# Seven products of combined quarters for the queries of a graph attention, and softmax sums turned by way of DRAM

## The chip, the core and the metric

The kernel runs on one core of one Trainium2 chip, in float32 throughout. The metric is the time on the device in microseconds (us), the median of several runs. A core has a matrix engine (PE, TensorE), a vector engine (DVE, VectorE), an engine for activation functions (ACT, ScalarE), a general engine (POOL, GpSimd) and one that here only issues DMA transfers (SP, SyncE). Each works through its own queue of instructions in order; semaphores tie them together. TensorE writes to PSUM, [...]from which VectorE and ScalarE read.

## The reference

There are 16 graphs (B) of 1024 nodes (N) with 256 channels (C), one 1024 x 1024 adjacency for all, and two layers with residuals. Cut to what matters:

```python
# layer 0: attention whose queries come from a weighted sum over neighbours
fea = transpose(relu(layernorm(x)))                     # (C, N) per graph
diff = c_adj[:, None, :] - c_adj[:, :, None]            # c_adj: mean over channels
A = abs(abs(sigmoid(diff) - 0.5) - 0.5) * 2.0           # symmetric
g = relu(einsum('bcn,bnm->bcm', fea, adj * A) * para)   # queries, 4 heads of 64
k, v = split((h @ kv_w))
x = x + softmax(q @ k.T * scale) @ v

# layer 1: graph convolution and two-layer perceptron with batch norms
deg = sum(A_norm, 0) + sum(A_norm, 1) - diagonal(A_norm)
agg = (A_norm * dinv[:, None] * dinv[None, :]) @ relu(layernorm(x))
y = relu(batchnorm(agg @ W1.T + b1))                    # over all graphs' nodes
x = x + batchnorm(y @ W2.T + b2)
```

The change concerns two places: the sum over neighbours `fea @ (adj * A)`, for each graph a product of 256x1024 by 1024x1024, and the division by the softmax's sums.

## The kernel before, in words

There are two stages. `layers` goes through the 16 graphs and ends with the perceptron's first half stored to DRAM (`y1_d`) and the residual (`x1_d`). `second` computes the batch norms over all graphs, the perceptron's second half and the output.

**One graph in the first stage.** `Norm` makes h_a, nodes on partitions, eight blocks of 128 nodes x 256 channels, and the channel sums csum. `columns_of` and `broadcast_row` spread those sums along a row (cbc, L181 to L193, called by `differences`). `transposed` makes ht, channels on partitions (L343 to L355). `weigh` (L363) makes the weighted adjacency in eight blocks w of 128 x 2 x 512: per block two Abs on ScalarE (L394), one Tanh (L402), and one operation on VectorE that adds one and multiplies with the block adj loaded from DRAM (L381). It is a generator of 17 slots; a block is spread over three of them. `queries` (L407) then takes, for each of two halves of 512 columns, 4 pairs of row blocks and 2 halves of channels, one piece each of four matmul instructions (`product`, L145 to L149: two half-width matmuls of 64 columns of weights). The sums of a column half gather in two PSUM banks, and are multiplied by para (L432) and put through relu (L435). `keys_values` makes keys and values from ht in eight pieces.

**Attention.** A unit is a pair of heads (k) and a half of the query nodes (f): four units per graph, 64 in all. A unit has four steps. Each step computes scores for two blocks of keys (L704), ScalarE's exponentials (L712), VectorE's running sum of the exponentials (acc, L731 and L734) and, one step later, the values' products o (L745). At a unit's end, two matmuls with a tile of ones (L762) sum acc over the partitions, with each head's sums repeated in 64 partitions; `divide` takes the reciprocals of that 128x512 tile in four pieces (L771) and multiplies with os, the copy of o (L774). Two steps later `finish` transposes os (L798), and adds it to the residual x (L802). Two reductions over the reciprocals (L777, L778) keep extremes in `seen`, from which the kernel tells whether a more careful version of the first stage (`layers(True)`) has to follow; it doesn't here.

**The order of the work.** `attention` writes it out by hand. Its 16 steps per graph are padded with pieces of other work from a generator, `background(b)`: while graph b attends, the queries, keys and values of graph b+1, the aggregation and the perceptron's first half of graph b-1, and the preparation of graph b+2 are issued. Every piece yields its cost in us of TensorE (1.71 for a piece), and after each step pieces are issued until the graph's `total` times the share of steps done is reached. `weave` puts one slot of a side generator behind each piece of the main one, `soon` puts an operation behind the next piece, and `TOP` stops until the scores of the next step are issued. `AHEAD` is the number of slots of `weigh` that are issued before the queries begin, in `prepare` three beside each of two groups of y pieces. `keys_values`, `queries`, `aggregate`, `hidden` and the transposes all take their PSUM from one pair of banks (`bank`, tag "mm").

`aggregate` (L489) already computes its product by seven products of combined quarters: fixed combinations of the normalized adjacency are made once, in `graph()` during graph 1, and kept in DRAM (`aht_d`); blocks of them are fetched three pieces ahead. `hidden` evicts the py banks to y on ScalarE (L564), stores y by a DMA that GpSimd issues (L565) and takes its statistics on VectorE (L568). `quarters` and `combine` (L474, L481) make two of the combinations of h_b.

**Buffers.** The pools are rings. There are four adj, w, p, q, k, v and y tiles, three of x and ht, two of acc, os, para and cb, and one of inv.

Of the kernel before, what the change touches and what calls it, by code (L numbers as in the profile page):

```python
# [17 lines left out]
P = 128  # L18
# [5 lines left out]
def gnn_two_layers_kernel(  # L24
# [36 lines left out]
    w2 = const.tile([P, HC, C], F32, name="w2")  # L61
# [11 lines left out]


# [10 lines left out]
    def layers(shifted):  # L85
# [12 lines left out]
        p3 = st.enter_context(tc.tile_pool(name=f"p3_{kind}", bufs=3))  # L98
        p4 = st.enter_context(tc.tile_pool(name=f"p4_{kind}", bufs=4))
# [41 lines left out]

        def bank(name):
            return ps_mm.tile([P, FB], F32, tag="mm", name=name)
# [15 lines left out]
        def load_adj(q, th, name):  # L159
            t = p4.tile([P, TH, FB], F32, tag="adj", name=name)  # L160
            nc.sync.dma_start(
                out=t,
                in_=adj[th * TH * P : (th + 1) * TH * P, q * FB : (q + 1) * FB].rearrange(
                    "(t p) m -> p t m", p=P
                ),
            )
            return t
# [4 lines left out]
        dbc = big.tile([P, N], F32, name="dbc")  # L172
        w1 = big.tile([P, CC, H1], F32, name="w1")
        rows = big.tile([P, NH, NT], F32, name="rows")

        def columns_of(col, name):

            cbs = []
            for g in range(NT // 4):
                cb = p2.tile([P, 4, P], F32, tag="cb", name=f"cb_{name}_{g}")  # L180
                nc.vector.tensor_copy(  # L181
                    cb, col[:, 4 * g : 4 * g + 4].unsqueeze(2).to_broadcast([P, 4, P])
                )
                cbs.append(cb)
# [10 lines left out]
        def load_adj_t(t, name):  # L195
            tile_ = p4.tile([P, N], F32, tag="adj", name=f"{name}_{t}")
# [3 lines left out]
        deg_sm = big.tile([P, 6, NT], F32, name="deg")  # L200
        row, diag, col, deg, tmp_deg, dinv = (deg_sm[:, i, :] for i in range(6))

        def degrees():

            nc.sync.dma_start(out=w1, in_=w1_t.rearrange("(k p) j -> p k j", p=P))
            nc.sync.dma_start(out=w2, in_=w2_t.rearrange("(k p) c -> p k c", p=P))
# [14 lines left out]
        def graph():  # L221
# [3 lines left out]
            for t in range(HT):  # L225
                for part in range(2):
                    cols = slice(part * HB, (part + 1) * HB)
                    a = p4.tile([P, 2, NH, HB], F32, tag="adj", name=f"au_{t}_{part}")
# [134 lines left out]
        def weigh(b):  # L363
# [11 lines left out]
            for slot in range(2 * NH * NP + 1):  # L375
# [11 lines left out]
                if not odd and i < NH * NP:  # L387
# [3 lines left out]
                    w = p4.tile([P, TH, FB], F32, tag="w", name=f"w_{b}_{q}_{th}")  # L391
# [13 lines left out]
        AHEAD = 6  # L405

        def queries(b):  # L407

            h = hs["a", b]
            qs[b] = [p4.tile([P, N], F32, tag="q", name=f"q_{b}_{k}") for k in range(CC)]  # L410
            for q in range(NH):
                cols = slice(q * FB, (q + 1) * FB)
                pgs = [bank(f"pg_{b}_{q}_{k}") for k in range(CC)]
                paras = []
                for k in range(CC):
                    paras.append(p2.tile([P, FB], F32, tag="para", name=f"para_{b}_{q}_{k}"))
                    nc.sync.dma_start(out=paras[k], in_=para[k * P : (k + 1) * P, cols])
                for th in range(NP):
                    i = q * NP + th
                    for k in range(CC):  # L420
                        for j in range(TH):
                            t = th * TH + j
                            product(
                                pgs[k],
                                h[:, t, k * P : (k + 1) * P],
                                weighted[b][i][:, j, :],
                                t == 0,
                                t == NT - 1,
                            )
                        if th == NP - 1:  # L430
                            dst = qs[b][k][:, cols]
                            nc.vector.tensor_mul(dst, pgs[k], paras[k])  # L432

                            soon(
                                lambda dst=dst: nc.scalar.activation(  # L435
                                    dst, dst, AF.Relu, scale=SCALE
                                )
                            )
                        yield 1.71
# [34 lines left out]
        def quarters(b):  # L474


            h = hs["b", b]
            HT = NT // 2
            return [h[:, n * HT : (n + 1) * HT, c * P : (c + 1) * P] for c in (0, 1) for n in (0, 1)]

        def combine(b):  # L481


            a11, a12, a21, a22 = quarters(b)
            s1s[b] = p1.tile([P, NT // 2, P], F32, tag="s1", name=f"s1_{b}")
            nc.vector.tensor_add(s1s[b], a21, a22)
            nc.vector.tensor_sub(a21, a11, a21)

        def aggregate(b):  # L489
# [5 lines left out]
            def load(upto):  # L495
                while len(pieces) <= min(upto, 7 * NP // 2 - 1):
                    i, th = divmod(len(pieces), NP // 2)
                    i = order[i]
                    a = p4.tile([P, TH, FB], F32, tag="adj", name=f"aht_{b}_{i}_{th}")
# [3 lines left out]
            load(2)  # L503
            yield 0.0
            a11, a12, a21, a22 = quarters(b)
            s1 = s1s[b]
# [18 lines left out]
            for i, (left, after) in enumerate(  # L525
# [11 lines left out]
                for th in range(NP // 2):  # L537
                    n = i * NP // 2 + th
                    load(n + 3)
# [35 lines left out]
        def normed(b):  # L575
# [3 lines left out]
            combine(b)  # L579
# [4 lines left out]
        def normed_last():  # L584
# [6 lines left out]
            combine(B - 1)  # L591
            nc.gpsimd.dma_start(out=x1_d[B - 1], in_=xs[B - 1])

        def prepare(b, products):
# [8 lines left out]
            for k in range(CC):  # L603
                yield from weave(islice(products, 3), (0, islice(w, 3)))
# [5 lines left out]
        endings = []  # L610

        def background(b):

            nothing = iter(())
            if b == 0:
                yield from prepare(1, nothing)
                yield from weave(queries(1), (0, weighers[1]), (1, degrees()))
                cbs = columns_of(dinv, "deg")
                if B > 2:
                    load_x(2)  # L620
                    yield from weave(keys_values(1), (1, Norm(2, True).all()))
                else:
                    yield from keys_values(1)
                yield TOP
                broadcast_row(dbc, cbs, "deg")
                yield 1.0
                if B > 2:
                    yield from prepare(2, nothing)
# [3 lines left out]
            if b + 1 < B:  # L632
                whole = graph() if b == 1 else nothing
                yield from weave(queries(b + 1), (0, weighers[b + 1]), (0, whole))
# [81 lines left out]
        class Unit:  # L716


            def __init__(self, b, k, f):
                self.at = (b, k, f)  # L720
                self.name = f"{b}_{k}_{f}"
                self.acc = None
                self.later = []
# [32 lines left out]
            def divide(self):  # L756

                b, k, f = self.at
                self.pt = ps_t.tile([P, FB], F32, tag="t", name=f"sums_{self.name}")
                for e in range(2):  # L760
                    r = slice(e * HD, (e + 1) * HD)
                    nc.tensor.matmul(  # L762
                        self.pt[r, :], ones, self.acc[:, e, :], start=True, stop=True
                    )
                self.inv = p1.tile([P, FB], F32, tag="inv", name=f"inv_{self.name}")
                u = (b * CC + k) * NH + f

                def invert(half):
                    for j in range(2 * half, 2 * half + 2):
                        c = slice(j * P, (j + 1) * P)  # L770
                        nc.vector.reciprocal(self.inv[:, c], self.pt[:, c])  # L771

                def scale():
                    nc.vector.tensor_mul(self.os, self.os, self.inv)  # L774

                def watch():
                    nc.vector.tensor_reduce(seen[:, 0, u : u + 1], self.inv, AX.X, ALU.max)  # L777
                    nc.vector.tensor_reduce(seen[:, 1, u : u + 1], self.inv, AX.X, ALU.min)  # L778

                invert(0)  # L780
                self.later = [lambda: invert(1), scale]
                self.watch = watch

            def behind_piece(self):
# [425 lines left out]
```

## Time and profile before

The median is 2698.26 us, of three runs from 2697.56 to 2699.33. The profiled execution spans 2698.1 us. What the chain that ended last consists of, by line:

| part of TensorE's work | line | share of the span |
|---|---|---|
| scores | L704 | 18% |
| values | L745 | 18% |
| queries (pg) | L149 | 16% |
| aggregation (pa) | L149 | 13% |
| perceptron, first half (py) | L149 | 7% |
| perceptron, second half (m_f) | L1017 | 7% |
| keys, values (pk, pv) | L149 | 4% each |
| sums, output's transposes | L762, L798 | 2%, 1% |

A group's line in the profile reads: line, engine, operation, output <- inputs with their shapes, count; busy us and mean ns of one; idle time of the engine just before them and what ended it. PE is TensorE, PEld its weight loads. A chain is followed back from the last instruction to what released each. In a table of windows each row gives a stretch of the span in us and the busy time of each engine in it.

Other durations that count: a row or column operation on 128x512 float32 takes VectorE 0.68 to 0.69 us, whether from PSUM or from SBUF; one on 128x1024 1.21 to 1.23; a ScalarE copy of 128x512 from PSUM 0.585, a pair of exponentials 1.94. The y stores land 2.8 us after their issue, the 512 KB adj blocks 4.2, the 1 MB yin blocks 6.3.

### The profile page before, as it was taken

What the parts mean: (1) busy time and instruction counts of PE and PEld (TensorE: products, weight loads), DVE (VectorE), ACT (ScalarE), POOL (GpSimd) and SP (SyncE); (2) the same over time, 40 slices, a digit from 0 to 9 for tenths busy, and PEclk for the clock granted to TensorE, in tenths of its full rate; (3) what the DMA queues carried; (4) which work ended last, traced back from release to release, by engine and by line L of the source; (5) the groups of instructions that cost most, each with busy time, mean ns of one, the idle gap of its engine ahead of it and who ended that gap; (6) DMA issues with size and microseconds to landing.
All of it is one profiled execution on the core that took longest, in us unless ns stands there. A gap on an engine that the chain in (4) does not pass through costs nothing.

```text
span 2698.1 us, 32021 instructions
## 1 busy us (share of the span) xinstructions
PE 2620.7 (97%) x12106; PEld 968.3 (36%) x12106; DVE 1742.3 (65%) x2624; ACT 1292.3 (48%) x1845; POOL 363.2 (13%) x428
## 2 busy tenths in 40 slices
PE   7999999999999999999999999999999999989994
PEld 3333333333333333333333333333333333324443
DVE  5767666666666656666666666566666666656675
ACT  5653444536363544445363635444453634335544
POOL 0016000000000100000000001000000001026653
PEclk9999999999999999999999999999999999999997
DMA  4416414243332424142423324241424213355549
GB/s 156 159 58 225 161 53 164 86 148 103 107 116 98 141 80 158 51 168 83 150 100 109 114 98 141 84 155 51 168 82 152 99 63 118 113 215 187 202 182 364
DMA packets 128613, 355.05 MB, mean 132 GB/s; under 512 B 11969, under 2 KB 32961, under 8 KB 122305
## 3 DMA queue, kind: packets, MB, share of 16 engines
q1 hardware_dynamic: 109120, 278.44, 30.3%
q0 software_dynamic: 19328, 74.46, 7.3%
q8 instruction: 98, 1.61, 0.2%
q14 instruction: 67, 0.54, 0.1%
HBM read 278.41 MB, written 74.45 MB: 131 GB/s over the span
## 4 chain that ended last, share of the span: by engine, by line
PE 93%; DMA 3%; DVE 2%; issue 2%; ACT 1%; POOL 0%; SPq 0%; POOLq 0%; DVEq 0%; ACTq 0%
PE sc L704 18%; PE o L745 18%; PE pg L149 16%; PE pa L149 13%; PE py L149 7%; PE m_f L1017 7%; PE pk L149 4%; PE pv L149 4%; PE sums L762 2%; DMA out_dram<-xo_f 2%; PE ot L798 1%; PE htp L352 1%; PE cbp_c L192 1%; DMA y_d<-y 0%; DVE acc L734 0%
## 5 line engine op out<-in xcount | busy, mean ns | idle before, releaser
L712 ACT ACTIVATE p<-sc 128x1024 f32<-128x1024 f32 x512 | 496.4, 1021 | 700.8 <-PE sc L704 700.6
L734 DVE TENSOR_TENSOR acc<-acc,p 128x1024 f32<-128x1024 f32 x384 | 471.2, 1227 | 133.8 <-ACT p L712 112.5
L704 PE MATMUL sc<-q,k 64*128 64x512 f32 x2048 | 510.6, 617 | 0.5 <-ACT p L712 0.5
L745 PE MATMUL o<-p,v 128*64 128x512 f32 x2048 | 496.1, 605 | 0.0
L149 PE MATMUL pg<-w,h_a 128*64 128x512 f32 x2048 | 457.1, 596 | 7.5 <-DVE q L432 7.5
L149 PE MATMUL pa<-aht,h_b 128*64 128x512 f32 x1536 | 346.0, 592 | 2.7 <-DMA aht<-aht_d 2.7
L704 PEld LDWEIGHTS sc<-q,k 64*128 64x128 f32 x2048 | 176.6, 186 | 321.9 <-issue 270.3
L149 PEld LDWEIGHTS pg<-w,h_a 128*64 128x64 f32 x2048 | 148.2, 138 | 301.8 <-issue 281.7
L771 DVE RECIPROCAL inv<-sums 128x128 f32<-128x128 f32 x256 | 223.7, 921 | 24.6 <-PE sums L762 24.6
L149 PE MATMUL py<-at,w 128*64 128x512 f32 x1024 | 230.8, 592 | 2.1 <-ACT y L564 2.1
L745 PEld LDWEIGHTS o<-p,v 128*64 128x64 f32 x2048 | 124.3, 136 | 286.1 <-issue 285.9
L394 ACT ACTIVATE w<-cbc,csum 128x512 f32<-128x512 f32 x256 | 170.2, 714 | 74.3 <-PE pg L149 74.2
L731 DVE TENSOR_TENSOR acc<-p,p 128x1024 f32<-128x1024 f32 x64 | 78.5, 1226 | 194.8 <-ACT p L712 194.8
L381 DVE SCALAR_TENSOR_TENSOR w<-w,adj 128x1024 f32<-128x1024 f32 x128 | 156.5, 1223 | 54.7 <-ACT w L402 54.7
L149 PEld LDWEIGHTS pa<-aht,h_b 128*64 128x64 f32 x1536 | 110.6, 137 | 216.6 <-issue 204.9
L564 ACT ACTIVATE y<-py,vec 128x512 f32<-128x512 f32 x128 | 87.6, 684 | 188.4 <-PE py L149 155.1
L565 POOL DMA_DIRECT2D y_d<-y x128 | 70.7, 553 | 685.1 <-ACT y L564 681.9
L402 ACT ACTIVATE w<-w 128x1024 f32<-128x1024 f32 x128 | 134.8, 1053 | 1.7
L149 PEld LDWEIGHTS py<-at,w 128*64 128x64 f32 x1024 | 74.0, 137 | 147.8 <-issue 131.3
L149 PE MATMUL pv<-kvw,ht 128*64 128x256 f32 x1024 | 116.2, 379 | 0.4 <-DVE v L469 0.4
L82 POOL TENSOR_SCALAR lnsm_b<-mv_b 128x4 f32<-128x4 f32 x32 | 7.3, 230 | 805.2 <-DVE mv_b L277 805.1
L802 DVE TENSOR_TENSOR x<-ot,x 128x512 f32<-128x512 f32 x64 | 44.2, 691 | 110.6 <-PE ot L798 109.8
(133 smaller groups left out, 2526.4 us busy)
## 6 DMA issues: line engine op xcount, KB each, us to landing
aht<-aht_d SPq DMA_DIRECT2D x224, 512.0 KB, 4.2
adj<-in_adj_dram SPq DMA_DIRECT2D x128, 512.0 KB, 4.2
y_d<-y POOLq DMA_DIRECT2D x128, 256.0 KB, 2.8
yin_f<-y_d SPq DMA_DIRECT2D x32, 1024.0 KB, 6.3
x<-in_x_dram SPq DMA_DIRECT2D x32, 512.0 KB, 4.7
para<-in_para_dram SPq DMA_DIRECT2D x64, 256.0 KB, 4.1
x_d<-x POOLq DMA_DIRECT2D x16, 1024.0 KB, 4.2
xo_f<-x_d SPq DMA_DIRECT2D x32, 512.0 KB, 8.5
```

What stands on the lines that cost most here:

```text
L149: nc.tensor.matmul(dst[r], left[:, r], right, start=start, stop=stop)
L381: nc.vector.scalar_tensor_tensor(w, w, 1.0, a, op0=ALU.add, op1=ALU.mult)
L394: nc.scalar.activation(w[:, t, :], cbc[:, q * FB : (q + 1) * FB], AF.Abs, bias=csum[:, th * TH + t : th * TH + t + 1], scale=-1.0,)
L402: nc.scalar.activation(made[i], made[i], AF.Tanh, scale=-0.5 / C)
L564: nc.scalar.activation(y, made, AF.Identity, bias=b1[:, j : j + 1])
L704: nc.tensor.matmul(sc[:, e, :], ks[b][k][r, m * P : (m + 1) * P], qs[b][k][r, f * FB : (f + 1) * FB], start=True, stop=True,)
L712: nc.scalar.activation(pr, sc, AF.Exp)
L731: nc.vector.tensor_add(self.acc, self.held, pr)
L734: nc.vector.tensor_add(self.acc, self.acc, pr)
L745: nc.tensor.matmul(self.o[r, :], vs[b][k][:, m, r], pr[:, e, :], start=(m == 0), stop=(m == NT - 1),)
L771: nc.vector.reciprocal(self.inv[:, c], self.pt[:, c])
L1017: nc.tensor.matmul(made, left[:, j, :], right[:, j, :], start=(j == 0), stop=(j == JH - 1))
```

## The change

It has two parts, and what they need of room.

**Queries by seven products.** With the 1024 nodes in two halves, and the 256 channels in two halves, `fea @ W` is a product of a 2x2 of quarters with a 2x2 of quarters, and can be had from seven products of sums and differences of quarters (Winograd's form of Strassen's product). The left sides are combined in place in h_a, the weights in place in the eight blocks of w (`take`), and the products are added up in q itself. All of that is done on VectorE, and two copies on ScalarE. All eight blocks of w have to be there at once, so their ring grows from four to eight (`p8`), the aggregation's blocks share it, and the adj ring shrinks to three. The blocks of w are made earlier: `AHEAD` grows from 6 to 9 slots, and `double` takes two slots behind each piece. For graph 0 all of them are made beside its keys and values. The order for graph 1 changes accordingly.

**Sums by way of DRAM.** ScalarE copies the 128x512 tile of sums to SBUF, GpSimd stores one row of it per head to DRAM, and two DMAs bring them back with query nodes on partitions, 128x4 per head. There the reciprocals are of 128x8, and they are applied after the output's transposes instead of before.

**Room.** dbc moves into the ring of ht, the cb tiles into that of y, and w2 is loaded at the start of `second` instead of at the first stage's start.

```diff
@@
-        w2 = const.tile([P, HC, C], F32, name="w2")
...
+        def double(slots):
+
+            for _ in slots:
+                next(slots, None)
+                yield 0.0
...
-            t = p4.tile([P, TH, FB], F32, tag="adj", name=name)
+            t = p3.tile([P, TH, FB], F32, tag="adj", name=name)
...
-                    w = p4.tile([P, TH, FB], F32, tag="w", name=f"w_{b}_{q}_{th}")
+                    w = p8.tile([P, TH, FB], F32, tag="w", name=f"w_{b}_{q}_{th}")
...
-        AHEAD = 6
+        AHEAD = 9
...
         def queries(b):
+            combine("a", b, nc.vector)
+            a11, a12, a21, a22 = quarters("a", b)
+            s1 = s1s["a", b]
...
+            def take(i, x, y, part):
+
+                nc.vector.tensor_sub(block(i)[part], block(x)[part], block(y)[part])
+
+            def first(m):
+                nc.scalar.copy(c12, m)
+                nc.scalar.copy(c21, m)
+                nc.vector.tensor_sub(a11, s1, a11)
+
+            def second(m):
+                add(c11, m, c12)
+                nc.vector.tensor_sub(a12, a12, a11)
+                soon(lambda: finish(0, 0))
...
+            for i, (left, right, midway, after) in enumerate(
+                (
+                    (a11, 0, (), first),
+                    (a12, 1, ((0, 2, 0, 0), (0, 2, 0, 1)), second),
+                    (s1, 0, (), third),
+                    (a12, 3, ((2, 3, 2, 1), (0, 3, 0, 0)), fourth),
+                    (a21, 2, ((0, 3, 0, 1), (1, 1, 0, 0)), fifth),
+                    (a11, 0, ((1, 1, 0, 1),), sixth),
+                    (a22, 1, (), seventh),
+                )
+            ):
...
         def prepare(b, products):
...
-                yield from weave(islice(products, 3), (0, islice(w, 3)))
+                yield from weave(islice(products, 3), (0, double(islice(w, AHEAD // 2 + k))))
...
-                yield from weave(queries(b + 1), (0, weighers[b + 1]), (0, whole))
+                sides = [(0, graph(whole.pop()))] if b == 1 else []
+                yield from weave(queries(b + 1), (0, double(weighers[b + 1])), *sides)
...
+                row = p1.tile([P, FB], F32, tag="row", name=f"row_{self.name}")
+                nc.scalar.copy(row, pt)
+                nc.gpsimd.dma_start(
+                    out=sums_d[u], in_=row.rearrange("(e r) c -> e r c", r=HD)[:, 0, :]
+                )
+                self.inv = p2.tile([P, FB // P, 2], F32, tag="inv", name=f"inv_{self.name}")
+                for e in range(2):
+                    nc.gpsimd.dma_start(
+                        out=self.inv[:, :, e], in_=sums_d[u][e].rearrange("(j q) -> q j", q=P)
                     )
...
             def finish(self):
...
+                nc.vector.reciprocal(self.inv, self.inv)
+                nc.vector.tensor_mul(
+                    self.os.rearrange("p (j e c) -> p j e c", j=J, e=2),
+                    pt.rearrange("p (j e c) -> p j e c", j=J, e=2),
+                    self.inv.unsqueeze(3).to_broadcast([P, J, 2, HD]),
+                )
                 dst = xs[b][:, f * J : (f + 1) * J, k * P : (k + 1) * P]
-                nc.vector.tensor_add(dst, pt.rearrange("p (j c) -> p j c", c=P), dst)
+                nc.vector.tensor_add(dst, self.os.rearrange("p (j c) -> p j c", c=P), dst)
...
-                        total = 41.0 * (b + 1 < B) + 24.0 * (b > 0) + 6.0 * (b + 2 < B)
+                        total = 37.6 * (b + 1 < B) + 24.0 * (b > 0) + 6.0 * (b + 2 < B)
...
-                run(weave(keys_values(0), (8 - AHEAD, islice(weighers[0], AHEAD))))
+                run(weave(keys_values(0), (0, double(weighers[0]))))
                 load_x(1)
-                run(weave(queries(0), (0, weighers[0]), (5, Norm(1, True).all())))
+                load_x(2)
+                run(weave(queries(0), (3, Norm(1, True).all())))
...
         with st:
+            w2 = wp.tile([P, HC, C], F32, name="w2")
+            nc.sync.dma_start(out=w2, in_=w2_t.rearrange("(k p) c -> p k c", p=P))
             JH = HC // 2
```

## The prediction

> **What bounds the kernel now.** I read the page's busy times first, then its chain and groups, then windows of the trace, and the waits last.
>
> ```profile
> PE 2620.7 (97%) x12106; PEld 968.3 (36%) x12106; DVE 1742.3 (65%) x2624; ACT 1292.3 (48%) x1845; POOL 363.2 (13%) x428
> ...
> PE 93%; DMA 3%; DVE 2%; issue 2%; ACT 1%; POOL 0%; SPq 0%; POOLq 0%; DVEq 0%; ACTq 0%
> ...
> L712 ACT ACTIVATE p<-sc 128x1024 f32<-128x1024 f32 x512 | 496.4, 1021 | 700.8 <-PE sc L704 700.6
> L734 DVE TENSOR_TENSOR acc<-acc,p 128x1024 f32<-128x1024 f32 x384 | 471.2, 1227 | 133.8 <-ACT p L712 112.5
> L149 PE MATMUL pg<-w,h_a 128*64 128x512 f32 x2048 | 457.1, 596 | 7.5 <-DVE q L432 7.5
> L771 DVE RECIPROCAL inv<-sums 128x128 f32<-128x128 f32 x256 | 223.7, 921 | 24.6 <-PE sums L762 24.6
> L394 ACT ACTIVATE w<-cbc,csum 128x512 f32<-128x512 f32 x256 | 170.2, 714 | 74.3 <-PE pg L149 74.2
> ```
>
> TensorE is busy 97% and owns 93% of the chain. The other engines have room on average, but only if their work falls where there is room, so I looked at windows (us, then busy time of PE, PEld, DVE, ACT, POOL; granted clock, DMA share, GB/s):
>
> ```profile
> 400.00:540.00 140.00, 140.00 (x676) 50.21 (x677) 90.45 (x128) 67.66 (x99) 8.80 (x15) 1.00 0.36 121
> ...
> 170.00:180.00 10.00, 5.59 (x34) 3.58 (x30) 6.00 (x9) 7.80 (x13) 0.00 (x0) 0.87 0.11 37
> 180.00:190.00 10.00, 10.00 (x38) 3.28 (x40) 5.40 (x7) 5.66 (x7) 0.00 (x0) 0.79 0.22 71
> 210.00:220.00 10.00, 5.05 (x12) 1.30 (x14) 8.09 (x10) 3.25 (x5) 7.36 (x8) 0.57 0.66 213
> ```
>
> In the loop TensorE has no idle time at all: every us of matmul removed there is a us gained, if no other engine becomes late. Around 170 to 220 us (graph 1, where the degree scaling and the DRAM combinations of the adjacency are made) it already waits for VectorE, and the clock dips too. The waits of PE and the loop's chain:
>
> ```profile
> PE pg L149 <- DVE q L432: 7.5, 3, 4.7
> ...
> PE htp L352 <- DVE ht L355: 3.8, 2, 3.5
> PE pa L149 <- DMA aht<-aht_d: 2.7, 2, 1.5
> ```
>
> ```profile
> 641.56 6.87 PE pg L149 x32
> 648.42 1.92 PE sc L704 x8
> 650.34 1.87 PE o L745 x8
> 652.21 5.15 PE pg L149 x24
> ```
>
> 24 records in 5.15 us are 0.2146 us each; 8 are a piece of 1.717 us. The same place in the loop returns each 148.28 us (493.29, 641.56, 789.82), one graph.
>
> **What the Trainium skill says.** "TensorE: Matmul & The Clock Gate", Part 1: a window of about 3.4 us of idleness halves the clock. The trace agrees: after the gap of 3.52 us at 178.02 the eight score matmuls took 3.79 us instead of 1.92. So a long stall costs more than its length. "DMA: Bandwidth & Descriptors", Anatomy of one DMA: some 2.0 us fixed plus bytes by 436 GB/s; the store of y (256 KB) gives 2.6, measured 2.8. Its Rules for kernel authors: a last dimension that isn't contiguous costs a descriptor per element, and a reading DMA must wait for the writing one's completion. No run here shows either yet. "SBUF — State Buffer", on its two sides: a VectorE operation on two SBUF inputs and GpSimd share a port. The new subtractions are of that kind; GpSimd is busy 8.8 us of 140 in the loop, so I cost that at nothing there.
>
> **The change, part by part.**
>
> *Queries.* Before, a graph has 2 column halves x 4 row blocks x 2 channel halves = 16 pieces; the seven products are two pieces each, 14. Two pieces fewer are 2 x 1.717 = 3.43 us per graph, 54.9 us for 16. This is all that TensorE gains: the sums' matmuls and the output's transposes stay.
>
> VectorE per graph, added: 2 combinations and 2 left subtractions of 128x512 (0.68 each, 2.75), 8 subtractions of 128x1024 (1.227, as L734: 9.8), 9 PSUM additions (0.69) plus 4 multiplications by para, for 4 before: +6.2. Sum +18.75. ScalarE gains 2 copies of 0.584 here and four row copies of 0.58 below: +3.5.
>
> *Sums.* Per unit VectorE loses 4 x 0.874 of reciprocal, 0.686 of multiplication and 1.345 of watching, 5.53; it gains a small reciprocal and two small reductions (0.16 each, as the 128x4 rows) and a multiplication of 0.69: 1.16. Four units: −17.5. So VectorE's total moves by only +1.3, from 96 to 97 of 145 us, and ScalarE from 74 to 78. But they move in time: the subtractions and the weights come in bursts.
>
> The trip: the row copy ends 5.3 us after the sums, the store lands about 2.8 later (as y_d), two issues of 0.55, and reading back. The reads are 512 elements of 4 bytes each, a kind that no row shows: between 2.6 us (a small DMA) and 10 (one descriptor per element over a few queues); I take 4. The reciprocal is due two attention steps on, at least 17 us after the sums: 5.3 + 2.8 + 1.6 + 4 = 14 is hidden, 20 is not. If it came late, the reciprocal would block VectorE's queue: behind it wait acc additions, then p buffers, exponentials and scores. I cost it at nothing except for the last unit, which nothing covers: −3 (1 to 6).
>
> *Queries in the loop.* Summing measured durations by attention step, PE/DVE/ACT in us: before 11.5/7.9/7.6, 8.9/6.3/6.0, 9.5/5.7/6.9; after 9.8/9.4/11.8, 8.9/9.6/3.7, 9.5/8.0/2.0, 8.9/7.1/2.0, 9.8/5.2/5.7. Nothing but the first step's ScalarE and the second's VectorE exceeds PE, and placing the subtractions in order against the products that need them leaves 1.8 us or more. So the 3.43 is realised here.
>
> *Preparation steps.* Twice as many slots of weights lie beside the y and ht pieces (`double`, AHEAD 9 for 6). This is where I see the loss. The timeline of before:
>
> ```profile
> 913.14 0.69 ACT L564 ACTIVATE y<-py,vec 128x512 f32<-128x512 f32 x1 [2.50 <-PE py L149]
> 913.73 1.32 ACT L394 ACTIVATE w<-cbc,csum 128x512 f32<-128x512 f32 x2
> ...
> 914.95 0.67 ACT L564 ACTIVATE y<-py,vec 128x512 f32<-128x512 f32 x1
> 915.52 1.05 ACT L402 ACTIVATE w<-w 128x1024 f32<-128x1024 f32 x1
> ```
>
> Each y eviction already stands behind half a block. After, a whole one (1.33 + 1.05 = 2.38) follows each, and 2.38 + 0.68 = 3.06 exceeds the piece's 1.717. With only two PSUM banks, the third product waits for the first's eviction, then the transposes for the second's and third's, then the exponentials of the next step start late. Laying the new order out with these durations gives stalls of 0.15, 0.55 and 0.65 us, and perhaps 0.3 where ht copies stand behind bn_stats: 1.35 per graph (0.7 to 2.6), for the 13 graphs with such steps −17.5 (9 to 34). The sums of the two steps go from 10.1/7.8/9.1 and 10.6/8.4/7.5 to 10.1/9.0/10.1 and 10.6/9.6/10.4: at the limit, not over.
>
> *Start.* All eight blocks of graph 0 precede its queries, by ScalarE's 2.38 each. My layout has the first scores at 66.1 instead of 61.9, though TensorE has 3.43 less to do: −7.7.
>
> *Graph 0's background.* Weights are made in the first pieces; step 3 has PE/DVE/ACT of 15.2/15.8/21.3. ScalarE exceeds by 6: −6 (2 to 12).
>
> *Graph 1.* Six steps sum to 55.8 of PE and 63.8 of VectorE (57.5 and 53.5 before), now with three adjacency buffers for four. 8 over, of which some was lost before already (9.9 us in gaps at 178, 213 and 218): −7 (3 to 16).
>
> *End.* Five pieces of aht are fetched ahead for three; the waits of 2.7 us above go: +2.7. But w2 is now loaded in the second stage. Its buffer was the layers', so SyncE waits for the last y stores and bn_stats; the four yin loads, which before were issued early,
>
> ```profile
> 2401.12 2.01 SPq L973 DMA_DIRECT2D yin_f<-y_d  x4
> ```
>
> stand behind it and come only at about 2417, with 6.3 us each. The first second-layer matmul (4.84 us of waiting at 2422.17 before) moves: −4.5 (2 to 8).
>
> *Sum:* 54.9 − 7.7 − 6 − 7 − 17.5 − 3 + 2.7 − 4.5 = 11.9; 2698.3 − 11.9 = 2686.
>
> **Rivals.**
> (A) The stalls are hidden: the engines' queues run ahead in the loop and absorb late evictions (in 400 to 540 us ScalarE is busy 48% only). Then only start, end and graph 1 cost, half of what I count: 54.9 − 14 = 41, 2657 to 2668. Against: two PSUM banks give PE little lead.
> (B) Slower: stalls at the upper ends, 2.6 per graph (34), 12, 16, 6 and 8, with 7.7 at the start: 83.7 − 2.7 − 54.9 = 26 lost, 2724; with some of them, 2704 to 2724. For: the waits of 7.5 us for VectorE exist, and the clock halves after long gaps. Against: the averages leave VectorE a third free.
> (C) Reading back takes 10 us or more: 20 − 17 = 3 us late per unit, 64 units: up to 190 less what the queues absorb. 2710 to 2880. Against: GpSimd is nearly idle, and the two steps between are usually nearer 20.
>
> **How the numbers follow.** Mine 0.46 (2672 to 2704), A 0.25, B 0.22, C 0.07. Faster by over 0.2% (below 2693): A and two thirds of mine, 0.56. Within: 0.15. Slower: B, C and what is left, 0.29. For 8 in 10 the range takes in A but for its best and the lower half of B: 2660 to 2714.
>
> **What would show it.** PE's sum falls by about 55 us to 2566. In the loop the period falls from 148.28 to about 146.2: 144.85 would say A, 147.5 or more B. PE's waits would then name y, ht or cbc evictions in prepare steps; waits on DVE q or on w in queries' steps would say that my placing there is wrong. First scores near 66. VectorE's waits show inv on a DMA only if C holds. The first yin issue after 2400 stands behind w2. I am wrong if TensorE's loop has no idle time (A), or if new waits stand in queries' steps.

## The result, and the profile after

The changed kernel takes 2713.6 us (median of 4, 2710.61 to 2715.54) against 2698.57: a ratio of 1.0055, 95% interval 1.0038 to 1.0072. It is slower by some 15 us, where 12 us faster was forecast. The profiled execution spans 2711.9 us.

From its page: busy times, chain, and the groups of the queries' products, of the weights and of the sums' reloads.

```profile
PE 2581.5 (95%) x11850; PEld 946.6 (35%) x11850; DVE 1748.7 (64%) x2768; ACT 1339.7 (49%) x1941; POOL 500.9 (18%) x620
...
PE 79%; ACT 6%; issue 5%; DVE 5%; DMA 3%; POOL 1%; ACTq 0%; POOLq 0%; SPq 0%; DVEq 0%
...
L156 PE MATMUL pg<-w,h_a 128*64 128x512 f32 x1536 | 346.1, 595 | 8.0 <-DVE w L461 5.7
L399 ACT ACTIVATE w<-cbc,csum 128x512 f32<-128x512 f32 x256 | 169.5, 712 | 0.0
L852 POOL DMA_DIRECT2D inv<-sums_d x128 | 98.4, 772 | 137.6 <-DMA sums_d<-row 73.9
```

With 256 products that read s_a, the queries have 1792 records, as counted. But TensorE's busy time fell by 39 us only, and it now has 130 us of idle time instead of 77. Its share of the chain fell from 93% to 79%, while ScalarE's rose from 1% to 6% and VectorE's from 2% to 5%. Where the time went is read from when the same work begins in both traces:

| from the start to | before, us | after, us | difference | gained (−) or lost in between |
|---|---|---|---|---|
| first scores | 61.9 | 70.0 | +8.1 | +8.1 |
| graph 2's first queries' product (graph 1's background begins) | 186.5 | 200.3 | +13.8 | +5.7 |
| graph 3's (graph 2's background) | 344.9 | 375.3 | +30.4 | +16.6 |
| graph 15's, twelve graphs on | 2124.1 | 2139.8 | +15.7 | −14.7 |
| end | 2698.1 | 2711.9 | +13.8 | −1.9 |

TensorE has 3.43 us less to do in each of the first three stretches and in the last, 41.2 less in the twelve graphs. So 11.5, 9.1, 20.0, 26.5 and 1.5 us of waiting came in. The last row but one is the loop: there the time from one graph's first queries' product to the next graph's, called the period below, fell from 148.27 us to 147.04 only. Windows of the changed kernel (as before: PE, PEld, DVE, ACT, POOL, clock, DMA share, GB/s), for the start, two parts of graph 1, and one graph of the loop:

```profile
24.00:70.00 46.00, 37.27 (x185) 14.30 (x183) 41.94 (x65) 23.48 (x43) 2.88 (x4) 0.93 0.36 121
...
200.30:250.00 49.70, 43.33 (x186) 13.64 (x185) 47.03 (x53) 19.67 (x26) 35.72 (x36) 0.97 0.61 196
...
264.00:285.00 21.00, 8.09 (x56) 4.08 (x56) 11.15 (x33) 4.60 (x8) 14.38 (x21) 0.79 0.54 167
...
522.30:669.30 147.00, 145.63 (x698) 51.55 (x696) 95.59 (x153) 74.28 (x109) 18.50 (x29) 1.00 0.33 115
```

The kernel before, for the first 50 us of graph 1 and for one graph of the loop:

```profile
186.50:236.20 49.70, 43.31 (x182) 13.49 (x180) 36.41 (x42) 20.96 (x26) 34.36 (x37) 0.90 0.59 199
...
493.29:641.56 148.27, 148.27 (x715) 52.91 (x712) 95.38 (x143) 71.21 (x104) 10.06 (x17) 1.00 0.34 114
```

At the start and in the first 50 us of graph 1 VectorE is busy 91% and 95% (73% in graph 1 before): it is the bound. In 264 to 285 no engine is: TensorE has a gap, and GpSimd is the busiest. In the loop TensorE idles 1.37 us per graph, and VectorE's 95.59 us are what it had before (95.38): the forecast of its net load held, and so did ScalarE's (71.2 to 74.3). What TensorE waited for, first over the whole span, then in that one graph:

```profile
PE pv L156 <- DVE lnsm_b L290: 12.9, 1, 12.9
PE m_f L1082 <- ACT yin_f L1044: 11.2, 1, 11.2
PE htp L357 <- ACT y L634: 10.5, 26, 0.6
PE pg L156 <- DVE w L461: 10.2, 6, 3.8
PE py L156 <- DVE ht L360: 7.4, 13, 0.6
```

```profile
PE htp L357 <- ACT y L634: 0.8, 2, 0.6
PE py L156 <- DVE ht L360: 0.6, 1, 0.6
```

The transposes wait for an eviction of y, 26 times in 13 graphs, and a y product for a copy of ht, 13 times: the preparation steps, in the form that the prediction described. The queries' own steps show no wait in the loop. The timeline of one preparation, cut to what matters:

```profile
495.94 1.32 ACT L399 ACTIVATE w<-cbc,csum 128x512 f32<-128x512 f32 x2
497.29 1.06 ACT L407 ACTIVATE w<-w 128x1024 f32<-128x1024 f32 x1
498.25 0.67 ACT L634 ACTIVATE y<-py,vec 128x512 f32<-128x512 f32 x1
...
498.82 1.32 ACT L399 ACTIVATE w<-cbc,csum 128x512 f32<-128x512 f32 x2
...
500.18 1.06 ACT L407 ACTIVATE w<-w 128x1024 f32<-128x1024 f32 x1
...
501.14 0.67 ACT L634 ACTIVATE y<-py,vec 128x512 f32<-128x512 f32 x1
501.71 1.93 ACT L794 ACTIVATE p<-sc 128x1024 f32<-128x1024 f32 x2
...
501.86 0.66 PE L357 MATMUL htp<-ident,h_a 128*128 128x128 f32 x4 [0.18 <-ACT y L634]
```

Between two y evictions (L634) stands a whole block of weights (L399 and L407), 2.4 us. The third eviction begins at 501.14, though its product was finished at about 498.7, when TensorE went on to the scores.

### The profile page after: what moved, and what is told of

The parts are those of the page before. It is cut to its first block, busy times and chain, and to the rows that moved or that the text cites. A ratio compares the mean times of both kernels' runs of the same rounds, so it can differ in the third digit from the quotient of the medians.

```text
span 2711.9 us, 32206 instructions
## 1 busy us (share of the span) xinstructions
PE 2581.5 (95%) x11850; PEld 946.6 (35%) x11850; DVE 1748.7 (64%) x2768; ACT 1339.7 (49%) x1941; POOL 500.9 (18%) x620
## 4 chain that ended last, share of the span: by engine, by line
PE 79%; ACT 6%; issue 5%; DVE 5%; DMA 3%; POOL 1%; ACTq 0%; POOLq 0%; SPq 0%; DVEq 0%
PE o L827 16%; PE sc L786 15%; PE pa L156 13%; PE pg L156 12%; PE m_f L1082 7%; PE py L156 4%; PE pv L156 4%; PE pk L156 3%; ACT w L399 3%; DMA out_dram<-xo_f 2%; PE sums L844 2%; ACT y L634 2%; PE ot L862 1%; DVE w L461 1%; PE cbp_c L197 1%
## 5 line engine op out<-in xcount | busy, mean ns | idle before, releaser
L156 PE MATMUL pg<-w,h_a 128*64 128x512 f32 x1536 | 346.1, 595 | 8.0 <-DVE w L461 5.7
L847 POOL DMA_DIRECT2D sums_d<-row x64 | 37.6, 587 | 1116.6 <-ACT row L846 1116.6
L156 PEld LDWEIGHTS pg<-w,h_a 128*64 128x64 f32 x1536 | 110.9, 137 | 229.4 <-issue 195.8
L399 ACT ACTIVATE w<-cbc,csum 128x512 f32<-128x512 f32 x256 | 169.5, 712 | 0.0
L634 ACT ACTIVATE y<-py,vec 128x512 f32<-128x512 f32 x128 | 87.1, 681 | 148.3 <-PE py L156 126.6
L461 DVE TENSOR_TENSOR w<-w,w 128x1024 f32<-128x1024 f32 x128 | 154.4, 1238 | 0.0
L407 ACT ACTIVATE w<-w 128x1024 f32<-128x1024 f32 x128 | 135.5, 1059 | 2.6
L156 PE MATMUL pv<-kvw,ht 128*64 128x256 f32 x1024 | 119.1, 384 | 17.2 <-DVE lnsm_b L290 12.9
L852 POOL DMA_DIRECT2D inv<-sums_d x128 | 98.4, 772 | 137.6 <-DMA sums_d<-row 73.9
```

The source lines that it names most:

```text
L156: nc.tensor.matmul(dst[r], left[:, r], right, start=start, stop=stop)
L399: nc.scalar.activation(w[:, t, :], cbc[:, q * FB : (q + 1) * FB], AF.Abs, bias=csum[:, th * TH + t : th * TH + t + 1], scale=-1.0,)
L407: nc.scalar.activation(made[i], made[i], AF.Tanh, scale=-0.5 / C)
L461: nc.vector.tensor_sub(block(i)[part], block(x)[part], block(y)[part])
L634: nc.scalar.activation(y, made, AF.Identity, bias=b1[:, j : j + 1])
L852: nc.gpsimd.dma_start(out=self.inv[:, :, e], in_=sums_d[u][e].rearrange("(j q) -> q j", q=P))
```

## Experiments

The trip is short for the sums' way through DRAM and back. Theories. **A**: the loop's loss is the burst of ScalarE's weights beside the y pieces; **B**: it comes with any such weights, or with the sums. For graph 1, **1**: GpSimd's queue, which holds the trip, the combinations of the adjacency and the reciprocal square roots of the norm; **2**: VectorE's load. **C**: the late start is graph 0's seven products, with all their weights made first.

**The trip's reloads later (fetch_late).** All but the last two units' reloads are issued one attention step later.

```diff
                         last.sums()
+                        if last.index < UNITS - 2:
+                            fetches.append(last)
...
+                while fetches:
+                    fetches.pop(0).fetch()
```

> The changed kernel, with the two reloads of the sums issued one attention step later (still by GpSimd), so that GpSimd's queue does not stand still until the store has landed. Theory 1 (in graph 1 GpSimd's queue, with the trip of the sums in it, makes the combinations and the reciprocal square roots late, and VectorE and then TensorE wait for those): the gap of 12.9 us falls below 8, the stretch from the first keys of graph 2 to the first aggregation, 44.6 us, falls to 28 to 38, the whole to 2697 to 2707. Theory 2 (VectorE itself is the bound there, through the subtractions and three adjacency buffers instead of four): stretch and total change by less than 3 us. Both: the period in the loop stays at 147.0.

2712.41 us, ratio 1.0047 (1.0031 to 1.0064) to before. TensorE's gap in graph 1 went from 12.9 to

```profile
PE pv L156 <- DVE lnsm_b L290: 9.6, 1, 9.6
```

but graph 2's first keys, ahead of it, came 2.3 us later, and graph 3's queries begin only 0.7 us earlier. The stretch from those keys to the first aggregation fell from 44.6 to 41.6 us, where theory 1 had 28 to 38. In graph 1 GpSimd's waits for the store fell from 12.2 to 1.4 us, but its waits for VectorE's scaled adjacency grew from 7.7 to 10.7. Theory 1 alone does not hold for the changed kernel.

**The trip on SyncE (sp_trip).** The same, with `nc.sync` for the store and the two reloads.

> As the run before, with the store and the reloads of the sums issued by SyncE, so that GpSimd has nothing of the trip in its queue. Theory 1: the stretch from graph 2's keys to the first aggregation falls to 22 to 30 us, the gap of 12.9 us to below 3, the whole to 2690 to 2701. Theory 2: less than 3 us of change. Period 147.0, unless SyncE's loads of adjacency come late behind the store's wait: then over 147.5.

2722.51 us, 1.0088 (1.0071 to 1.0105): 9 us slower than the changed kernel and 10 slower than fetch_late. Of those 10 us, 9 are lost in graph 1, where the reload now stood behind five loads of aht in SyncE's queue and VectorE waited for it:

```profile
DVE inv L869 <- DMA inv<-sums_d: 10.4, 1, 10.4
```

The period stayed 147.0. Both theories' numbers were missed: the edit moved the wait to another queue, so it does not decide between them.

**Fewer weights ahead (ahead7).** AHEAD 7; 3 slots singly, then 4 doubled; one subtraction moved back.

```diff
-        AHEAD = 9
+        AHEAD = 7
...
-                    (a12, 1, ((0, 2, 0, 0), (0, 2, 0, 1)), second),
+                    (a12, 1, ((0, 2, 0, 0),), second),
...
-                yield from weave(islice(products, 3), (0, double(islice(w, AHEAD // 2 + k))))
+                ahead = islice(w, 3 + k)
+                yield from weave(islice(products, 3), (0, double(ahead) if k else ahead))
```

> The changed kernel with AHEAD 7 instead of 9: 3 slots of weights, not doubled, beside the first three y pieces and 4 doubled beside the next three; one subtraction moves behind the second product, so that the weights it needs may come later. Theory A (the loop's loss of 2.2 us against the 3.43 that TensorE saves is ScalarE's burst of weights beside the y pieces, behind which evictions of two PSUM banks stand): the period falls from 147.02 to 145.0 to 146.2 us and the total by 10 to 25, to 2689 to 2704. Theory B (the loss comes with the interruptions by transposes and scores, or with the sums, and not from the burst): the period stays within 0.3 of 147.0. If the weights now come late for the queries, waits for w appear in their steps and the period rises above 147.3.

2745.67 us, 1.017 (1.0153 to 1.0187). One graph of its loop, and TensorE's waits in it:

```profile
526.50:676.30 149.80, 146.91 (x700) 52.01 (x698) 95.88 (x153) 74.01 (x109) 18.46 (x29) 0.99 0.33 113
```

```profile
PE pg L156 <- DVE w L461: 2.6, 1, 2.6
PE htp L357 <- ACT y L635: 0.3, 1, 0.3
```

The waits of the preparation steps fell from 1.4 to 0.3 us, as A says (so did the number of slots, so that "any such weights" is not excluded), but the queries now waited 2.6 us for their weights, and each graph took 149.6 on average. The total missed both theories' numbers; the last sentence of the expectation is what happened. Seven slots are too few; the question is how the nine lie.

**The same nine slots, spread (even9).**

```diff
-                yield from weave(islice(products, 3), (0, double(islice(w, AHEAD // 2 + k))))
+                yield from weave(islice(products, 3), (0, islice(w, 3)), (0, islice(w, 1)))
                 yield TOP
                 transposed(b, k)
                 yield 1.0
-            yield from products
+            yield from weave(products, (0, islice(w, 1)))
```

> The changed kernel with the same nine slots of weights before the queries, spread over the preparation's seven y pieces as 2, 1, 1 and 2, 1, 1 and 1 instead of doubled (2, 2, 0 and 2, 2, 1 and 0). Theory A (the loop's loss is ScalarE's burst of weights in front of evictions that free the two PSUM banks): the period falls from 147.02 to 145.4 to 146.4 us and the total from 2713.6 to 2693 to 2707. Theory B (any weights there delay the evictions alike, only their number counts): the period stays within 0.3 us of 147.0.

2686.83 us, ratio to before 0.996 (0.9947 to 0.9972): 27 us faster than the changed kernel, with period and total both better than the expected ranges. A graph of its loop:

```profile
516.30:661.20 144.90, 144.90 (x698) 51.68 (x696) 95.47 (x153) 73.91 (x109) 18.46 (x29) 1.00 0.35 117
```

TensorE has no idle time, with the same ScalarE and VectorE work in the graph. The period is 144.93 us, against 148.27 − 3.43 = 144.84. And the transposes follow without a wait, because ScalarE now has half a block between evictions:

```profile
494.91 1.32 ACT L399 ACTIVATE w<-cbc,csum 128x512 f32<-128x512 f32 x2
...
496.14 0.67 ACT L634 ACTIVATE y<-py,vec 128x512 f32<-128x512 f32 x1
...
496.70 1.05 ACT L407 ACTIVATE w<-w 128x1024 f32<-128x1024 f32 x1
...
497.17 1.04 PE L357 MATMUL htp<-ident,h_a 128*128 128x128 f32 x8
```

A holds and B falls: the number of slots is the same, and so are the sums. All but 0.1 us of the loop's loss is how the slots were doubled.

**Graph 0's queries direct (start_direct).** Its 16 pieces and their weights in the order of before, all later graphs by seven products.

```diff
-                run(weave(keys_values(0), (0, double(weighers[0]))))
+                run(weave(keys_values(0), (2, islice(weighers[0], 6))))
...
-                run(weave(queries(0), (3, Norm(1, True).all())))
+                run(weave(queries_direct(0), (0, weighers[0]), (5, Norm(1, True).all())))
```

> The changed kernel with graph 0's queries as one direct product in 16 pieces, with weights and loads in the order of the kernel before; all later graphs by seven products. Theory C (the later start is the making of all weights and the combinations ahead of the queries): first scores at 61.5 to 63 instead of 70.0, and the total 5 to 9 us lower, 2704 to 2709. Rival (graph 0's background is bound by ScalarE and VectorE, so an earlier start is given back there): the start moves as much, but the first queries' product of graph 1's background is less than 4 us earlier than in the changed kernel, and the total within 4 us.

2704.55 us, 1.0025 (1.0016 to 1.0035), 9 us less than the changed kernel; first scores at 62.46, and graph 2's queries 11.7 us earlier. C holds, and graph 0's background gives nothing back. The start's window, beside the one above of 24 to 70:

```profile
24.00:62.46 38.46, 36.96 (x203) 15.18 (x199) 26.74 (x45) 25.79 (x45) 2.53 (x4) 1.00 0.57 192
```

The same advance of the work takes VectorE 26.7 us instead of 41.9. ScalarE does 25.8 us of work in this shorter time, more than the 23.5 of the changed kernel, so ScalarE was not what held that one back.

**And graph 2's queries direct (direct02).** `queries_direct` for those too, which are made in graph 1's background.

> As start_direct, and graph 2's queries, which are made during graph 1 beside the combinations of the adjacency, also as one direct product in 16 pieces; all other graphs by seven products. Theory 2 (in graph 1 VectorE is the bound, by the subtractions and additions on top of the scaling of the adjacency, and what GpSimd does follows late from that): the stretch from graph 2's first keys to the first aggregation falls from 44.6 to 22 to 32 us, and the total from 2704.6 to 2686 to 2697. Theory 1 (GpSimd's chain of combinations, trip and reciprocal square roots is the bound whatever VectorE does): the stretch stays above 38 and the total above 2700.

2689.53 us, 0.9969 (0.9958 to 0.9981): 15 us below start_direct, although TensorE has 3.43 us more to do. Graph 1's background, first the queries, then from graph 2's keys to the first aggregation:

```profile
189.10:245.60 56.50, 51.20 (x218) 16.42 (x218) 39.26 (x47) 22.88 (x29) 41.94 (x49) 0.94 0.71 229
245.60:269.60 24.00, 22.48 (x136) 9.79 (x133) 15.53 (x39) 10.39 (x17) 14.07 (x19) 1.00 0.61 208
```

The second stretch fell from 44.6 to 24.0 us, with the trip still in GpSimd's queue and still three adjacency buffers. Theory 2 holds: graph 3's queries begin 13.6 us earlier than in start_direct, so the seven products cost 17.0 us of waiting in graph 1, by VectorE's work. The gap of 12.9 us in the changed kernel is where this arrived: late scaling by VectorE, late combinations on GpSimd, behind them the norm's square root, for which VectorE's queue stood 9.4 us, and then the values' products:

```profile
DVE lnsm_b L290 <- POOL lnsm_b L83: 9.4, 1, 9.4
```

```profile
268.30 3.62 PE L156 MATMUL pv<-kvw,ht 128*64 128x256 f32 x32
284.84 3.68 PE L156 MATMUL pv<-kvw,ht 128*64 128x256 f32 x16 [12.91 <-DVE lnsm_b L290]
```

Behind the gap 16 records take as long as 32 did ahead of it; the granted clock in 264 to 285 is 0.79. Up to the gap little is lost: the first six steps of graph 1 take 68.4 us, where the kernel before took 69.8 with 3.43 us more of TensorE's work; the seventh takes 24.4 instead of 9.5.

A second thing in the changed kernel's trace makes both engines later. VectorE operations with both inputs in SBUF and GpSimd's combinations stretch each other when they run together. The subtraction of weights takes 1.22 us in the 121 cases that meet no GpSimd operation, up to 1.76 in graph 1; a combination (L252) takes 0.73 once VectorE is idle, up to 1.6 before:

```profile
246.31 1.75 DVE L461 TENSOR_TENSOR w<-w,w 128x1024 f32<-128x1024 f32 x1
...
252.94 1.60 POOL L252 TENSOR_TENSOR two<-au,two 128x256 f32<-128x256 f32 x1
...
268.08 0.73 POOL L252 TENSOR_TENSOR two<-au,two 128x256 f32<-128x256 f32 x1
```

The additions that read one input from PSUM (L488) keep their 0.68 us beside GpSimd. Summed over graph 1's background this is, by estimate from these durations, 9 us of VectorE's time (5 before) and 13 of GpSimd's. How much of the gap it makes was not tried.

**Each part alone (sums_only, products_only).** The kernel before with the sums' trip; the changed kernel with the old division.

> The kernel before with only the sums by way of DRAM; queries, weights and buffers as before. Both theories: TensorE's work in the loop is untouched, so the period stays at 148.26 within 0.1, and VectorE's busy time falls by some 17 us per graph. Theory 1 (the trip in GpSimd's queue hurts graph 1): 5 to 15 us slower than before, all of it before the third graph. Theory 2 (it doesn't): within 5 us of before.

2703.16 us, 1.002 (1.0012 to 1.0029): some 5 us slower, on the border of the two expectations. The period is 148.3; of 4.8 us in the trace 4.0 are lost in graph 1's background, 0.5 ahead of it. GpSimd's wait there:

```profile
POOL inv L771 <- DMA sums_d<-row: 7.5, 2, 3.8
```

So the trip is hidden in the loop and at the end, and in graph 1 theory 1 is right where VectorE isn't the bound (sums_late, below, tests it).

> The changed kernel with the division of before (four reciprocals of 128x128, multiplication, two reductions on VectorE per unit). VectorE then has some 113 us per graph instead of 96, and at the first steps of the queries up to 13.6 us in a step in which TensorE has 9.8. If that lateness reaches TensorE: period 148 to 152 us, total 2725 to 2780, which would show what the sums' part is for. If VectorE's queue absorbs it: period within 0.3 of 147.0 and total within 6 us of the changed kernel.

2717.77 us, 1.0069 (1.0052 to 1.0085). The period is 147.46, 0.42 more than with the trip and so just outside the second case; the total is as near to the changed kernel as that case says. VectorE's 15.6 us more per graph (111.3 against 95.6) are almost absorbed, even with the weights in bursts. This run also parts the two theories on graph 1: with no trip in any queue, the stretch from graph 2's keys to the first aggregation is still 38.4 us (with the division's work on VectorE besides), against 44.6 with the trip and 24.0 in direct02.

**Sums alone, reloads later (sums_late).** sums_only with the edit of fetch_late.

> sums_only (the kernel before with only the sums by way of DRAM) with the two reloads issued one attention step later. If the standing of GpSimd's queue until the store has landed (7.5 us of waits for it in graph 1 there) makes the 4.9 us that sums_only is slower than the kernel before: 2697 to 2700. If it is something else (the issues themselves, VectorE's order at a unit's end): 2702 to 2705.

2699.6 us, 1.0005 (0.9996 to 1.0014). The standing queue is most of what sums_only lost by: 3.6 of its 5 us come back. A step later the store has landed, and the 7.5 us are gone.

**w2 early (w2_kvw).** w2 goes into the buffer of kvw, which nothing reads after graph 15's values.

```diff
+    kvw = const.tile([P, CC, 2 * C], F32, name="kvw")
+    w2 = kvw.rearrange("p k (a c) -> p (k a) c", c=C)
...
+            if b == B - 1:
+                load_w2()
```

> The changed kernel with w2 loaded into the buffer of kvw (same size, last read for graph 15's values) at the start of graph 15, so that at the start of the second stage nothing stands before the yin loads in SyncE's queue. If the queue behind w2 costs what was forecast at the end: the wait of 11.2 us for the first normalized yin falls below 6 and the total by 2 to 8 us, to 2706 to 2712. If the first matmul of the second stage is held by the last stores and statistics anyway: the total changes by less than 2 us. Loop and start as in the changed kernel.

2707.02 us, 1.0034 (1.0021 to 1.0046), 6.6 us less than the changed kernel. The end of the first stage in the changed kernel's chain:

```profile
2423.44 2.36 DMA y_d<-y
...
2425.94 0.38 SPq L1015
...
2426.38 6.17 DMA yin_f<-y_d
...
2432.65 0.82 ACT yin_f L1044
```

Store, SyncE's queue, yin's load, as forecast. With w2 early the chain goes from the last store through the square root (0.73) to ScalarE, and no load of yin is in it; the wait, just over the 6 us of the expectation, is

```profile
PE m_f L1087 <- ACT yin_f L1049: 6.1, 1, 6.1
```

**Together (all_three, old_division).** even9, direct02 and w2_kvw; then the same with the old division.

> The changed kernel with the three edits together: weights spread 2, 1, 1 and 2, 1, 1 and 1, graphs 0 and 2 with direct queries, w2 in the buffer of kvw. If the causes are independent, the differences measured alone add up: 2713.6 - 26.8 - 24.1 - 2 to 8 = 2655 to 2661. If an earlier start is given back anywhere, 2664 or more. Period 144.9.

2657.82 us, 0.9848 (0.9832 to 0.9865): the causes add up.

> As all_three, with the division of before (reciprocals of 128x128 on VectorE) instead of the sums by way of DRAM. If the sums' part makes room on VectorE that the seven products need: period 145.3 to 147 and 6 to 30 us slower than all_three. If, with the weights spread evenly, VectorE has room enough: period within 0.2 of 144.9 and the total within 6 us of all_three, perhaps below it by up to 5 us, which the sums' part alone cost on the kernel before.

2651.84 us, 0.9828 (0.9812 to 0.9845): a further 6 us less without the trip, 1 us more than the outer edge of the expectation; in the traces 5 of them lie before graph 3's queries. Its loop:

```profile
440.00:580.00 140.00, 140.00 (x675) 49.90 (x671) 107.14 (x157) 70.51 (x104) 10.02 (x17) 1.00 0.33 116
```

VectorE carries 107 of 140 us, and TensorE has no idle time: a period of 144.83 us. That is the fastest version here, 46 us below before. Fourteen graphs times 3.43 are 48. All three edits with the trip kept and its reloads a step later were not run.

## Why the prediction was wrong, point by point

Two terms of its sum carry most of the error: graph 1 was put at 7 us and lost 17.8, because the prediction compared VectorE's sum with TensorE's and did not follow what waits behind VectorE; the preparation steps were put at 17.5 us and lost some 28.7, because only the gaps were counted.

- **What TensorE saves: right.** 3.43 us per graph; the two versions with spread weights show the whole of it in the period.
- **VectorE and ScalarE in total: right** (per graph of the loop +1.3 forecast, about +0.2 measured; +3.5 and +3.0). So was the queries' loop: no wait in those steps.
- **Preparation steps: right in mechanism, too small in size.** Forecast 1.35 us per graph, measured 2.2, or 11 us more over 13 graphs. The layout's stalls were nearly exact: 1.37 us idle, in three gaps of 0.18, 0.57 and 0.62. But TensorE's busy time per graph is 145.63 us instead of even9's 144.90. Another 0.73 lies inside the durations: four transposes take 0.60 us, and the four after the gap 0.66, where eight in a row take 1.04. Stalls were added as gaps alone.
- **Start: right in direction, wrong engine.** Forecast "by ScalarE's 2.38 each", first scores at 66.1; it was VectorE, with the weights, graph 0's row sums, the combinations and subtractions in one queue, and 70.0. The loss was 11.5 us, for 7.7 forecast.
- **Graph 0: 9.1 for 6**, within the range given. 4.1 of it goes when the start is direct; with it TensorE's waits for ScalarE's exponentials fall there from 6.5 to 2.9 us. A wait of 4.5 us for VectorE (cb_deg) stays. The rest was not tried.
- **Graph 1: the step that failed most.** "8 over, of which some was lost before already: −7". The loss was 20.0, of which 2.2 are its preparation step. The sum of VectorE's work was right: in the six steps VectorE is busy 62.2 us (51.9 before), and 63.8 was forecast. What the step left out is what waits behind VectorE: the combinations on GpSimd, and behind these the norm's square root, which VectorE itself then awaits. So VectorE's lateness came back to VectorE itself by way of GpSimd, as the gap of 12.9 us, and it cost once more in the clock behind the gap. The prediction named what is queued behind the sums' reciprocal, but not what is queued behind VectorE here, since it took GpSimd as "nearly idle": true in the loop, and false in this one graph, where GpSimd is busy 35.7 of the first 49.7 us. For the same reason it put the port that two-input VectorE operations and GpSimd share at nothing, from the loop, and left it out of graph 1.
- **The trip: right for the loop** (rival C fell; VectorE never waited for inv there); **wrong for the last unit**, costed at 3 us: sums_only is 4.8 us behind at graph 15's queries and 4.8 at the end. In graph 1, where it was put at nothing, it costs 4.0 on the kernel before.
- **End: right.** w2's queue cost 6.6 us by the medians and 4.7 by the two traces, for 4.5; the aht waits did vanish.
- **The rivals.** The time came out in the middle of B's 2704 to 2724. B's cause, engines late in preparation and graph 1, is the one seen, but not in B's sizes: graph 1 lost more than B's 16 and the start more than its 7.7, the last unit nothing. A's absence of stalls is what even9 then produced by another order of the same work.

Terms by size, against the forecast: graph 1 without its preparation 11 us more (17.8 for 7), preparation 11, start 4 and graph 0 3 more, the last stretch 3 less (1.5 for 4.8): 26 us, which is the whole way from 12 us faster to the 14 slower that the two traces show.

## What to carry to other kernels

When a matmul saving is paid for with work on other engines, lay that work out in small pieces between the evictions that free PSUM; here slots doubled behind each piece cost some 60% of the saving in the loop, with averages unchanged. Look for the stages where the other engines aren't idle, here graph 1 and the start, and leave the old form there. And test by itself a part that only makes room: with the weights spread, the room that the sums' trip made was not needed.

## What the runs showed of the hardware that was not expected

VectorE operations on two SBUF inputs and GpSimd's operations slowed each other where they ran together: 1.22 us became up to 1.76 on VectorE, 0.73 up to 1.6 on GpSimd, while VectorE operations with an input in PSUM kept their 0.68.

The reload of 512 elements of 4 bytes, out of line in DRAM, took 4.1 us from issue to landing in the changed kernel and 2.7 in sums_only. Whether each element has a descriptor of its own, as the prediction quotes from the Trainium skill ("DMA: Bandwidth & Descriptors", Rules for kernel authors), no run here shows: the trace counts packets, 16 of 128 bytes for each reload, and 32 elements lie in each.

Three short idle gaps cost more than they show, though the clock stayed at 1.00: 1.37 us of gaps per graph went with 0.73 us of longer busy time for the same instructions, and the period differs by their sum, 2.1 us.
